# Layer-0 scores taken from x with joined weights, masks on GpSimd, and a reordered front and middle, in a two-layer graph kernel

## The chip, the cores and the metric

The kernel runs on one core of one Trainium2 chip, in float32 throughout. The metric is the device time of one launch in microseconds (us), the median of three runs. The engines are named as in the profile: PE (TensorE matmul), PEld (its weight load), DVE (VectorE), ACT (ScalarE), POOL (GpSimd), SP (SyncE, which here only issues DMAs).

## What is computed

There are 16 batches of N = 1024 nodes with D = 128 features, x and a dense adjacency matrix adj of zeros and ones, symmetric, with ones on its diagonal. Two layers follow each other, each with a residual and a layer norm. Cut to what matters:

```python
# layer 0
h = x @ Ww.T + Wb
e = (h @ A) @ h.T ;  e = e + e.T                 # = h (A + A.T) h.T
scores = where(adj > 0, e, 0)
attention = softmax(scores, axis=1) * adj
hp = relu(attention @ h)
ic, fc, oc = (sigmoid(hp @ w_u + x @ w_x) for each gate)
x = layernorm(x + oc * tanh(ic * hp + fc * x))
# layer 1, 4 heads
h = x @ conv_w + conv_b
Ah = tanh(adj * (h @ attn_w @ h.T))
hh = relu(Ah @ h)                                # per head
x = layernorm(x + relu(relu(mean over heads of hh) + x))
```

## The kernel before, in words

Features lie on the 128 partitions in the transposed tensors (xT, hT, gT, hpT, x1T, uT: 128 x 1024), nodes in the others. A block of 128 nodes against all 1024 nodes is one 128 x 1024 tile; each is made as two matmuls of 128 x 512 (q = 0, 1), and each such matmul is two passes of TensorE in the profile, so "x4" in the trace is one tile.

Nothing is rescheduled by a planner: every engine runs its own queue in the order in which the code emits instructions. That order is written by hand. A batch of layer 1 has 32 **steps**, numbered here 0 to 31 as `hd * NB + m` (head times 8 plus block). A step m of `layer1_step` issues two score matmuls (L358), the two multiplications with adj on DVE (L359) and one tanh on ACT (L360). The two matmuls that add the tile to the head's output (L364, "back") are kept in a queue and issued DELAY = 2 steps later. After a head's last block the output is added to a running sum on DVE (L374 and L376), which falls in the second step of the next head, and the next head's first accumulation must wait for that.

Layer 0 of the next batch, `layer0(b + 1)`, is a generator that runs inside these steps: at each step listed in BETWEEN one part of it is issued, up to its next `yield`. BETWEEN holds steps 1 to 27 without step 4. The last stage of the batch before, `layer1_end(b - 1)`, is a second generator: its first part is issued in step 3 (transposes L386, y on DVE L389 and L393, the statistics of `layernorm` L157 to L161 on DVE and the power on POOL L162) and its second part in step 4 (normalisation L165 on DVE, output DMA L395 on the POOL queue). Within a step the order is: layer 1, then the part of `layer1_end`, then the part of `layer0`.

So layer 0 in the kernel before runs as: step 1 hT (`project_T`), step 2 h with three gate columns (L218, L219), step 3 gT = a_sym hT (`project_T`, L174), then `front(j)` in step 5 + 2j and `middle(j)` with `back(j - 1)` in step 6 + 2j, the last `back` and the relu in step 21, gates in 22, u in 23 (L297 to L305), L311 and the statistics in 24, normalisation in 25.

`front(j)`: two score matmuls (L236), mask and multiply on DVE (L237), row maximum on DVE (L242), exp on ACT (L244), multiplication with adj on POOL (L245). `middle(j)`: the reciprocal of the sums (L252) and hz = h / sums (L254), both on DVE. `back(j)`: two accumulating matmuls (L260).

For batch 0 there is no layer 1 to run beside, so its layer 0 runs alone at the start of the kernel (the prologue).

PSUM has two accumulators of 128 x 1024 and one pool `ps_sc` of four 128 x 512 buffers under one tag, "sc". Every other PSUM tile (layer 1 scores, layer 0 scores, projections, transposes) takes the next of these four in turn, so each waits until the tile four places before it has been read. In SBUF the layer-0 tiles `s0` have three buffers, and adj tiles 17.

Of the kernel before, what the change touches and what calls it, by code (L numbers as in the profile page):

```python
# [10 lines left out]
F32 = mybir.dt.float32  # L11
AF = mybir.ActivationFunctionType
ALU = mybir.AluOpType
# [3 lines left out]
P = 128  # L17
# [4 lines left out]
def two_layer_adjacency_kernel(  # L22
# [19 lines left out]
    nc = tc.nc  # L42
    B, N, D = x.shape
    H = conv_w.shape[0]
    assert D == P and N % 512 == 0
    NB = N // P
# [3 lines left out]
    consts = ctx.enter_context(tc.tile_pool(name="consts", bufs=1))  # L50
    adjp = ctx.enter_context(tc.tile_pool(name="adjp", bufs=2 * NB + 1))
    sb = ctx.enter_context(tc.tile_pool(name="sb", bufs=2))
# [4 lines left out]
    def small(name):  # L57
        return ps_sc.tile([P, 512], F32, tag="sc", name=name)


    ident = consts.tile([P, P], F32, name="ident")
# [4 lines left out]
    ww_in = consts.tile([P, P], F32, name="ww_in")  # L66
    nc.sync.dma_start(ww_in, Ww)
    a_in = consts.tile([P, P], F32, name="a_in")
    nc.sync.dma_start(a_in, A)
    wb_col = consts.tile([P, 1], F32, name="wb_col")  # L70
    nc.sync.dma_start(wb_col, Wb.rearrange("(d o) -> d o", o=1))

    G = D + 3
    KG = 512 // G
    GROUPS = [range(k, min(k + KG, NB)) for k in range(0, NB, KG)]
    wwT_g = consts.tile([P, G], F32, name="wwT_g")
    ident_g = consts.tile([P, G], F32, name="ident_g")
    wwT = wwT_g[:, :D]
    nc.gpsimd.tensor_copy(ident_g[:, :D], ident)
    wb_row = consts.tile([P, G], F32, name="wb_row")  # L80
    nc.gpsimd.memset(wb_row[:, D:G], 0.0)
    nc.sync.dma_start(wb_row[:, :D], Wb.partition_broadcast(P))
    gate_u, gate_x = ident_g[:, D:G], wwT_g[:, D:G]

    for t, ws in ((gate_x, (wi_x, wf_x, wo_x)), (gate_u, (wi_u, wf_u, wo_u))):
        for g, w in enumerate(ws):
# [20 lines left out]
    caT = consts.tile([P, H, P], F32, name="caT")  # L107
    ms = consts.tile([P, H, P], F32, name="ms")

    a_sym = consts.tile([P, P], F32, name="a_sym")  # L110
    pw = small("pw")
    nc.tensor.transpose(pw[:, :P], ww_in, ident)
    nc.tensor.transpose(pw[:, P : 2 * P], a_in, ident)
    nc.scalar.copy(wwT, pw[:, :P])
    nc.vector.tensor_add(a_sym, pw[:, P : 2 * P], a_in)

    def join_weights():

# [51 lines left out]
    def project_T(dst, w, src, bias, name):  # L170

        for q in range(NH):
            ps = small(f"pT_{name}_{q}")
            nc.tensor.matmul(ps, w, src[:, ts(q, 512)], start=True, stop=True)  # L174
            if bias is None:
                nc.scalar.copy(dst[:, ts(q, 512)], ps)  # L176
            else:
                nc.scalar.activation(dst[:, ts(q, 512)], ps, AF.Identity, bias=bias)
# [13 lines left out]
    adj_t, x_t, x1_t = {}, {}, {}  # L192


    def layer0(b):

        xTb = sb.tile([P, N], F32, tag="xT", name=f"xT_{b}")
        nc.sync.dma_start(xTb, xT[b])
        adj_t[b] = []
        for j in range(NB):  # L200
            t = adjp.tile([P, N], F32, tag="adj", name=f"adj_{b}_{j}")
            nc.sync.dma_start(t, adjT[b, ts(j, P), :])
            adj_t[b].append(t)
            if j == 0:
                xb = sb.tile([P, NB, D], F32, tag="x", name=f"x_{b}", bufs=1)
                nc.sync.dma_start(xb, x[b].rearrange("(k p) d -> p k d", p=P))
                if b == 0:
                    load_late_weights()

        hT = sb.tile([P, N], F32, tag="hT0", name=f"hT0_{b}", bufs=1)  # L210
        gT = sb.tile([P, N], F32, tag="gT0", name=f"gT0_{b}", bufs=1)
        h = sb.tile([P, NB, G], F32, tag="h0", name=f"h0_{b}", bufs=1)
        project_T(hT, wwT, xTb, wb_col, f"h0_{b}")
        yield
        for ks in GROUPS:
            ps = small(f"pR_h0_{b}_{ks[0]}")[:, : len(ks) * G].rearrange("p (k d) -> p k d", d=G)
            for i, k in enumerate(ks):
                nc.tensor.matmul(ps[:, i, :], xTb[:, ts(k, P)], wwT_g, start=True, stop=True)  # L218
            nc.vector.tensor_add(  # L219
                h[:, ks[0] : ks[-1] + 1, :], ps,  # L220
                wb_row.unsqueeze(1).to_broadcast([P, len(ks), G]),
            )
        yield

        project_T(gT, a_sym, hT, None, f"g0_{b}")
        yield

        acc = ps_acc.tile([P, N], F32, tag="acc0", name=f"acc0_{b}")
        held = {}

        def front(j):

            s = sb.tile([P, N], F32, tag="s0", name=f"s0_{b}_{j}", bufs=3)
            for q in range(NH):
                ps = ps_sc.tile([P, 512], F32, tag="sc", name=f"sc0_{b}_{j}_{q}")
                nc.tensor.matmul(ps, hT[:, ts(j, P)], gT[:, ts(q, 512)], start=True, stop=True)  # L236
                nc.vector.scalar_tensor_tensor(  # L237
                    s[:, ts(q, 512)], adj_t[b][j][:, ts(q, 512)], 0.0, ps,
                    op0=ALU.is_gt, op1=ALU.mult,
                )  # L240
            nmax = sb.tile([P, 1], F32, tag="nmax", name=f"nmax_{b}_{j}", bufs=4)
            nc.vector.tensor_reduce(nmax, s, AX.X, ALU.max, negate=True)  # L242
            z = sb.tile([P, 1], F32, tag="z", name=f"z_{b}_{j}", bufs=4)
            nc.scalar.activation(s, s, AF.Exp, bias=nmax, accum_out=z)  # L244
            nc.gpsimd.tensor_mul(s, s, adj_t[b][j])  # L245
            held[j] = s, z

        def middle(j):

            s, z = held[j]  # L250
            rz = sb.tile([P, 1], F32, tag="rz", name=f"rz_{b}_{j}", bufs=4)
            nc.vector.reciprocal(rz, z)  # L252
            hz = sb.tile([P, D], F32, tag="hz", name=f"hz_{b}_{j}", bufs=4)
            nc.vector.tensor_scalar_mul(hz, h[:, j, :D], rz)  # L254
            held[j] = s, hz

        def back(j):
            s, hz = held.pop(j)
            for q in range(NH):
                nc.tensor.matmul(  # L260
                    acc[:, ts(q, 512)], hz, s[:, ts(q, 512)],
                    start=(j == 0), stop=(j == NB - 1),
                )


        for j in range(NB):
            front(j)
            yield
            middle(j)
            if j:  # L270
                back(j - 1)
            yield
        back(NB - 1)

        hpT = sb.tile([P, N], F32, tag="hpT", name=f"hpT_{b}", bufs=1)
        for q in range(NH):
            nc.scalar.activation(hpT[:, ts(q, 512)], acc[:, ts(q, 512)], AF.Relu)
        yield


        hp = sb.tile([P, NB, G], F32, tag="hp", name=f"hp_{b}", bufs=1)
        for ks in GROUPS:
            pt = small(f"pt0_{b}_{ks[0]}")[:, : len(ks) * G].rearrange("p (k d) -> p k d", d=G)
            for i, k in enumerate(ks):
                nc.tensor.matmul(pt[:, i, :], hpT[:, ts(k, P)], ident_g, start=True, stop=True)  # L285
            nc.scalar.copy(hp[:, ks[0] : ks[-1] + 1, :], pt)

        gate = sb.tile([P, NB, 3], F32, tag="gate", name=f"gate_{b}")
        gflat = gate.rearrange("p k g -> p (k g)")
        nc.vector.tensor_add(gate, hp[:, :, D:G], h[:, :, D:G])  # L290
        nc.scalar.activation(gflat, gflat, AF.Exp, scale=-1.0)
        nc.vector.tensor_scalar_add(gflat, gflat, 1.0)
        nc.vector.reciprocal(gflat, gflat)
        yield

        u = sb.tile([P, NB, D], F32, tag="u", name=f"u0_{b}", bufs=1)
        nc.gpsimd.tensor_mul(u, xb, gate[:, :, 1:2].to_broadcast([P, NB, D]))  # L297
        for q in range(NH):
            for i in range(BH):
                k = q * BH + i  # L300
                nc.vector.scalar_tensor_tensor(  # L301
                    u[:, k, :], hp[:, k, :D], gate[:, k, 0:1], u[:, k, :],
                    op0=ALU.mult, op1=ALU.add,
                )
            nc.scalar.activation(  # L305
                u[:, q * BH : (q + 1) * BH, :], u[:, q * BH : (q + 1) * BH, :], AF.Tanh
            )
        yield

        for k in range(NB):  # L310
            nc.vector.scalar_tensor_tensor(  # L311
                u[:, k, :], u[:, k, :], gate[:, k, 2:3], xb[:, k, :], op0=ALU.mult, op1=ALU.add
            )

        x1 = sb.tile([P, NB, D + 1], F32, tag="x1", name=f"x1_{b}")
        nc.gpsimd.memset(x1[:, :, 0:1], 1.0)
        yield from layernorm(u, x1[:, :, 1 : D + 1], f"0_{b}")
        x1_t[b] = x1
# [77 lines left out]


    first, join = layer0(0), None
    for step, _ in enumerate(first):
        if step == 3:  # L400
# [80 lines left out]
```

## Time and profile before

| what | value |
|---|---|
| median of three runs | 2664.63 us (2664.5 to 2665.58) |
| the profiled execution | 2664.39 us, its span 2662.6 us |
| PE busy | 2581.3 us, 97% of the span |
| DVE busy | 1650.3 us, 62% |
| ACT busy | 961.5 us, 36% |
| POOL busy | 402.0 us, 15% |
| chain that ended last | PE 86%, DVE 6%, issue 2%, POOL 1%, ACT 1% |

The span is the time from the first to the last instruction of the profiled execution. The chain that ended last is followed back from the last instruction, at each step to what released it. A busy PE is not PE at its peak, since the ends of matmuls are modelled, so the step from one matmul to the next in the chain is the better price of a matmul than the "mean ns of one".

### The profile page before, as it was taken

Reading aid. Unit: us, or ns where it says so; the run is one execution under the profiler, and the core shown is the slowest. Engines: PE = TensorE matmul, PEld = TensorE weight load, DVE = VectorE, ACT = ScalarE, POOL = GpSimd, SP = SyncE. Lnnn points to the kernel's source line nnn. Section 1 sums busy time; section 2 is a strip of 40 time slices with the busy share of each in tenths; the row PEclk is TensorE's granted clock in tenths of the full one; section 3 lists DMA queues with packets and bytes.
Section 4 is the critical chain, followed back from the end, with each engine's and each line's share of the span. In section 5 each row is a group of like instructions: output and inputs, shape, how many; then the busy total and the mean of one; then the engine's idle time right before and its main releaser. Section 6 shows DMA issues by size and latency. Waiting matters only on the chain.

```text
span 2662.6 us, 19095 instructions
## 1 busy us (share of the span) xinstructions
PE 2581.3 (97%) x6552; PEld 1187.3 (45%) x6552; DVE 1650.3 (62%) x2994; ACT 961.5 (36%) x1253; POOL 402.0 (15%) x219
## 2 busy tenths in 40 slices
PE   6799999999999999999999999999999999999997
PEld 3344444444444444444444444444444444444443
DVE  5475765747666575665747757476565756657454
ACT  2334334343333333333343343433333343333432
POOL 2120110202112021120201102021120211202000
PEclk9899999999999999999999999999999999999999
DMA  3202001020110202002020010201102020020000
GB/s 106 79 0 79 9 29 58 1 79 8 54 34 0 79 8 71 16 0 87 0 79 8 24 63 0 79 8 48 40 0 79 8 72 16 0 71 0 0 8 8
DMA packets 42264, 94.23 MB, mean 35 GB/s; under 512 B 3894, under 2 KB 21686, under 8 KB 42167
## 3 DMA queue, kind: packets, MB, share of 16 engines
q1 hardware_dynamic: 38999, 84.62, 9.7%
q0 software_dynamic: 2304, 8.39, 1.1%
q8 instruction: 51, 0.84, 0.1%
q14 instruction: 46, 0.38, 0.0%
q10 hardware_dynamic: 864, 0.00, 0.0%
HBM read 84.61 MB, written 8.39 MB: 35 GB/s over the span
## 4 chain that ended last, share of the span: by engine, by line
PE 86%; DVE 6%; issue 2%; POOL 1%; ACT 1%; POOLq 0%
PE acc L364 29%; PE sc L358 28%; PE sc L236 8%; PE acc L260 8%; PE pT_u L174 4%; PE pR L337 4%; DVE s L359 1%; DVE u L301 1%; DVE u L311 1%; POOL u L297 1%; PE pR_h L218 1%; PE pT_g L174 1%; PE pT_h L174 1%; DVE st L157 1%; PE pt L285 1%
## 5 line engine op out<-in xcount | busy, mean ns | idle before, releaser
L359 DVE TENSOR_TENSOR s<-sc,adj 128x512 f32<-128x512 f32 x1024 | 687.1, 687 | 603.3 <-PE sc L358 588.1
L364 PE MATMUL acc<-s,h 128*128 128x512 f32 x2048 | 963.3, 593 | 26.4 <-DVE sum L376 26.4
L358 PE MATMUL sc<-uT,x1T 128*128 128x512 f32 x2048 | 962.5, 593 | 0.5 <-DVE s L359 0.5
L360 ACT ACTIVATE s<-s 128x1024 f32<-128x1024 f32 x512 | 541.2, 1057 | 1029.1 <-DVE s L359 1028.0
L364 PEld LDWEIGHTS acc<-s,h 128*128 128x128 f32 x2048 | 388.5, 190 | 520.4 <-issue 481.0
L358 PEld LDWEIGHTS sc<-uT,x1T 128*128 128x128 f32 x2048 | 386.4, 190 | 467.8 <-issue 417.9
L245 POOL TENSOR_TENSOR s<-s,adj 128x1024 f32<-128x1024 f32 x128 | 301.2, 2353 | 1006.4 <-ACT s L244 885.8
L244 ACT ACTIVATE s<-s,nmax 128x1024 f32<-128x1024 f32 x128 | 147.0, 1149 | 445.7 <-DVE nmax L242 445.7
L254 DVE TENSOR_SCALAR hz<-h,rz 128x128 f32<-128x128 f32 x128 | 270.3, 2111 | 4.5
L237 DVE SCALAR_TENSOR_TENSOR s<-adj,sc 128x512 f32<-128x512 f32 x256 | 172.1, 685 | 162.6 <-PE sc L236 152.3
L260 PE MATMUL acc<-s,hz 128*128 128x512 f32 x512 | 245.6, 603 | 12.6 <-DVE hz L254 12.5
L236 PE MATMUL sc<-gT,hT 128*128 128x512 f32 x512 | 240.7, 593 | 0.0
L162 POOL TENSOR_TENSOR rs<-rs,mhalf 128x8 f32<-128x8 f32 x32 | 52.8, 1651 | 1005.4 <-DVE rs L161 1005.4
L260 PEld LDWEIGHTS acc<-s,hz 128*128 128x128 f32 x512 | 98.0, 193 | 137.3 <-issue 121.0
L242 DVE TENSOR_REDUCE nmax<-s 128x1 f32<-128x1024 f32 x128 | 156.2, 1220 | 4.4
L236 PEld LDWEIGHTS sc<-gT,hT 128*128 128x128 f32 x512 | 97.8, 191 | 123.4 <-issue 122.2
L174 PE MATMUL pT_u<-x1T,ms 128*128 128x512 f32 x256 | 121.9, 599 | 0.0
L337 PE MATMUL pR<-cw,x1T 128*128 128x512 f32 x256 | 114.9, 593 | 0.0
L340 ACT COPY h<-pR 128x512 f32<-128x512 f32 x128 | 75.0, 586 | 48.6 <-PE pR L337 48.6
L376 DVE SCALAR_TENSOR_TENSOR sum<-acc,sum 128x512 f32<-128x512 f32 x96 | 61.7, 685 | 37.2 <-PE acc L364 37.2
L176 ACT COPY uT<-pT_u 128x512 f32<-128x512 f32 x128 | 71.3, 581 | 21.5 <-PE pT_u L174 21.5
L174 PEld LDWEIGHTS pT_u<-x1T,ms 128*128 128x128 f32 x256 | 49.1, 192 | 61.2 <-issue 53.3
(70 smaller groups left out, 868.3 us busy)
## 6 DMA issues: line engine op xcount, KB each, us to landing
adj<-in_adjT_dram SPq DMA_DIRECT2D x128, 512.0 KB, 3.7
xT<-in_xT_dram SPq DMA_DIRECT2D x16, 512.0 KB, 4.3
x<-in_x_dram SPq DMA_DIRECT2D x16, 512.0 KB, 4.3
out_dram<-y POOLq DMA_DIRECT2D x16, 512.0 KB, 3.9
aw<-in_L_gnn_attn_w_dram SPq DMA_DIRECT2D x1, 256.0 KB, 4.9
cw_in<-in_L_gnn_conv_w_dram SPq DMA_DIRECT2D x1, 254.0 KB
ww_in<-in_L_gnn_Ww_dram SPq DMA_DIRECT2D x1, 64.0 KB, 2.2
a_in<-in_L_gnn_A_dram SPq DMA_DIRECT2D x1, 64.0 KB, 2.4
```

Source lines behind the costliest of these rows:

```text
L174: nc.tensor.matmul(ps, w, src[:, ts(q, 512)], start=True, stop=True)
L236: nc.tensor.matmul(ps, hT[:, ts(j, P)], gT[:, ts(q, 512)], start=True, stop=True)
L237: nc.vector.scalar_tensor_tensor(s[:, ts(q, 512)], adj_t[b][j][:, ts(q, 512)], 0.0, ps, op0=ALU.is_gt, op1=ALU.mult,)
L242: nc.vector.tensor_reduce(nmax, s, AX.X, ALU.max, negate=True)
L245: nc.gpsimd.tensor_mul(s, s, adj_t[b][j])
L254: nc.vector.tensor_scalar_mul(hz, h[:, j, :D], rz)
L260: nc.tensor.matmul(acc[:, ts(q, 512)], hz, s[:, ts(q, 512)], start=(j == 0), stop=(j == NB - 1),)
L337: nc.tensor.matmul(ps, x1T_t[b][:, ts(k, P)], cw.rearrange("p h d -> p (h d)"), start=True, stop=True)
L358: nc.tensor.matmul(ps, x1T[:, ts(m, P)], uT[:, ts(q, 512)], start=True, stop=True)
L359: nc.vector.tensor_mul(s[:, ts(q, 512)], ps, adj[:, ts(q, 512)])
L360: nc.scalar.activation(s, s, AF.Tanh)
L364: nc.tensor.matmul(acc[:, ts(q, 512)], h1[:, ts(hd, D)], s[:, ts(q, 512)], start=(m == 0), stop=(m == NB - 1),)
```

## The change

Layer 0's scores are written as x Q x.T with Q = Ww.T (A + A.T) Ww and two bias terms. With c = Ww.T (A + A.T) Wb, the part that runs along the columns goes into qT = Q xT + c as a bias per partition, and the part that is one number per row (c.x + Wb.(A + A.T)Wb) is carried as a fourth extra column of h. Q and c are made once, in the prologue, with two more rounds of small matmuls. hT and gT go; qT is the only projected transpose.

In the scores the mask is no longer made in the DVE instruction. `mask(j)` makes it on POOL, as adj > 0 into the tile s itself, and DVE then computes (scores + row number) * mask. `mask(0)` is emitted with `front(0)`; `mask(j + 1)` is emitted inside `front(j)`, ahead of the POOL multiplication of tile j. `front(j + 1)` is emitted ahead of `middle(j)`. hz is made on ACT in place of DVE. s0 has four buffers, hpT shares the buffer of qT.

Because the gT part is gone, layer 0 now runs one part earlier: step 1 qT, step 2 h, step 3 `mask(0)` and `front(0)`, then `front(j)` in step 3 + 2j for j of 1 and more, `middle(j)` in step 6 + 2j (the last in step 19), the last `back` and the relu in step 20, gates in 21, u in 22, L311's work in 23, normalisation in 24. BETWEEN is as it was.

```diff
-    G = D + 3
+    G = D + 4
...
+    nc.gpsimd.memset(ident_g[:, D:G], 0.0)
...
-    gate_u, gate_x = ident_g[:, D:G], wwT_g[:, D:G]
+    gate_u, gate_x = ident_g[:, D : D + 3], wwT_g[:, D : D + 3]
...
-    nc.tensor.transpose(pw[:, :P], ww_in, ident)
-    nc.tensor.transpose(pw[:, P : 2 * P], a_in, ident)
-    nc.scalar.copy(wwT, pw[:, :P])
-    nc.vector.tensor_add(a_sym, pw[:, P : 2 * P], a_in)
+    nc.tensor.transpose(pw[:, :P], a_in, ident)
+    nc.tensor.transpose(pw[:, P : 2 * P], ww_in, ident)
+    nc.vector.tensor_add(a_sym, pw[:, :P], a_in)
+    nc.scalar.copy(wwT, pw[:, P : 2 * P])
+    nc.vector.tensor_copy(b_wide, wb_col.to_broadcast([P, P]))
+    pw2 = small("pw2")
+    nc.tensor.matmul(pw2[:, :P], a_sym, ww_in, start=True, stop=True)
+    nc.tensor.matmul(pw2[:, P : P + 1], a_sym, wb_col, start=True, stop=True)
+    nc.vector.tensor_copy(s_ww, pw2[:, :P])
+    nc.vector.tensor_copy(sb_col, pw2[:, P : P + 1])
+    pw3 = small("pw3")
+    nc.tensor.matmul(pw3[:, :P], s_ww, ww_in, start=True, stop=True)
+    nc.tensor.matmul(pw3[:, P : P + 1], s_ww, wb_col, start=True, stop=True)
+    nc.tensor.matmul(pw3[:, P + 1 : P + 2], b_wide, sb_col, start=True, stop=True)
+    nc.vector.tensor_copy(q_w, pw3[:, :P])
+    nc.vector.tensor_copy(c_col, pw3[:, P : P + 1])
+    nc.vector.tensor_copy(wwT_g[:, G - 1 : G], pw3[:, P : P + 1])
+    nc.vector.tensor_copy(wb_row[:, G - 1 : G], pw3[:, P + 1 : P + 2])
...
-        hT = sb.tile([P, N], F32, tag="hT0", name=f"hT0_{b}", bufs=1)
-        gT = sb.tile([P, N], F32, tag="gT0", name=f"gT0_{b}", bufs=1)
+        qT = sb.tile([P, N], F32, tag="qT0", name=f"qT0_{b}", bufs=1)
...
-        project_T(hT, wwT, xTb, wb_col, f"h0_{b}")
+        project_T(qT, q_w, xTb, c_col, f"q0_{b}")
...
-        project_T(gT, a_sym, hT, None, f"g0_{b}")
-        yield
-
...
+        def mask(j):
+
+            s = sb.tile([P, N], F32, tag="s0", name=f"s0_{b}_{j}", bufs=4)
+            nc.gpsimd.tensor_scalar(s, adj_t[b][j], 0.0, None, ALU.is_gt)
+            held[j] = s
+
         def front(j):
 
-            s = sb.tile([P, N], F32, tag="s0", name=f"s0_{b}_{j}", bufs=3)
+            s = held[j]
...
-                nc.tensor.matmul(ps, hT[:, ts(j, P)], gT[:, ts(q, 512)], start=True, stop=True)
+                nc.tensor.matmul(ps, qT[:, ts(j, P)], xTb[:, ts(q, 512)], start=True, stop=True)
                 nc.vector.scalar_tensor_tensor(
-                    s[:, ts(q, 512)], adj_t[b][j][:, ts(q, 512)], 0.0, ps,
-                    op0=ALU.is_gt, op1=ALU.mult,
+                    s[:, ts(q, 512)], ps, h[:, j, G - 1 : G], s[:, ts(q, 512)],
+                    op0=ALU.add, op1=ALU.mult,
                 )
...
             nc.scalar.activation(s, s, AF.Exp, bias=nmax, accum_out=z)
+            if j + 1 < NB:
+                mask(j + 1)
             nc.gpsimd.tensor_mul(s, s, adj_t[b][j])
...
-            nc.vector.tensor_scalar_mul(hz, h[:, j, :D], rz)
+            nc.scalar.mul(hz, h[:, j, :D], rz)
...
+        mask(0)
+
+
+        front(0)
+        yield
         for j in range(NB):
-            front(j)
-            yield
+            if j + 1 < NB:
+                front(j + 1)
+                yield
             middle(j)
             if j:
                 back(j - 1)
             yield
         back(NB - 1)
 
-        hpT = sb.tile([P, N], F32, tag="hpT", name=f"hpT_{b}", bufs=1)
+        hpT = sb.tile([P, N], F32, tag="qT0", name=f"hpT_{b}", bufs=1)
...
-        nc.vector.tensor_add(gate, hp[:, :, D:G], h[:, :, D:G])
+        nc.vector.tensor_add(gate, hp[:, :, D : D + 3], h[:, :, D : D + 3])
```

## The prediction

> **What bounds the kernel now.** I read the page first, then the windows of single batches, then the timeline of the steps that the change touches. The page's slices and chain, and the three groups that the change moves or queues behind:
>
> ```profile
> PE   6799999999999999999999999999999999999997
> ...
> PE 86%; DVE 6%; issue 2%; POOL 1%; ACT 1%; POOLq 0%
> ...
> L245 POOL TENSOR_TENSOR s<-s,adj 128x1024 f32<-128x1024 f32 x128 | 301.2, 2353 | 1006.4 <-ACT s L244 885.8
> ...
> L254 DVE TENSOR_SCALAR hz<-h,rz 128x128 f32<-128x128 f32 x128 | 270.3, 2111 | 4.5
> ...
> L162 POOL TENSOR_TENSOR rs<-rs,mhalf 128x8 f32<-128x8 f32 x32 | 52.8, 1651 | 1005.4 <-DVE rs L161 1005.4
> ```
>
> After the first two slices PE never leaves 9. One batch period in the windows (us, PE, PEld, DVE, ACT, POOL, clock, DMA):
>
> ```profile
> 1392.70:1554.50 161.80, 160.04 (x409) 73.70 (x408) 103.04 (x187) 59.88 (x79) 25.04 (x13) 1.00 0.11 36
> ```
>
> PE is idle 1.76 us in 161.8, all in one place: the last head's first accumulation waits for the sum (L376). So a batch is a row of matmuls, at 1.72 us per tile of two 512-wide ones (the chain, from one tile to the next). A matmul removed is time saved; DVE, ACT and POOL cost nothing until they hold PE up. The timeline of steps 3 to 5, where the change puts its first mask:
>
> ```profile
> 1411.37 1.88 PE L174 MATMUL pT_g<-hT,a_sym 128*128 128x512 f32 x4
> ...
> 1415.94 0.17 DVE L161 TENSOR_SCALAR rs<-mv 128x8 f32<-128x8 f32 x1
> 1416.02 1.29 DVE L359 TENSOR_TENSOR s<-sc,adj 128x512 f32<-128x512 f32 x2
> 1416.19 1.64 POOL L162 TENSOR_TENSOR rs<-rs,mhalf 128x8 f32<-128x8 f32 x1 [52.13 <-DVE rs L161]
> 1416.52 1.88 PE L358 MATMUL sc<-uT,x1T 128*128 128x512 f32 x4
> 1417.86 2.14 DVE L165 TENSOR_SCALAR y<-y,mv,rs 128x128 f32<-128x128 f32 x8 [0.55 <-POOL rs L162]
> ```
>
> Start, duration, engine. Today POOL's power lies under two layer-1 multiplications: only L165 waits for it, 0.55 us. PE at 1416.52 already begins step 5; it is a full step ahead of DVE.
>
> **What the skill says.** "SBUF — State Buffer", section "Who interferes with whom": VectorE's two-port forms (tensor_scalar among them) and GpSimd exclude each other for a whole instruction, and whichever began first keeps the port. The trace agrees: hz (L254) takes 0.29 us at its shortest and 2.28 at the median, and one that began 0.86 us into a POOL multiplication ended 0.08 us after it (1426.10 + 1.57 against 1425.24 + 2.35). "GPSIMD Engine Reference", section 3.1, gives a two-input operation 2.6 cycles an element at 1.2 GHz, which is 2.22 us for 1024; L245 shows 2.35, so 0.13 are fixed. It gives a simple one-input body 1.03 cycles; no run here shows a one-input operation of that size.
>
> **The change, part by part.**
>
> *gT goes.* Batches 1 to 15 each lose one tile of matmuls: 15 x 1.72 = **25.8 us off**. The two 128x131 groups (1.79 us each a batch) grow by 1/131: 16 x 2 x 0.014 = 0.4 on. Together **-25.4**. One ACT copy pair goes, and is off the path.
>
> *hz to ACT.* It frees DVE of 270 us and costs ACT 128 x about 0.27 (the 128x128 copy at L114 took 0.265). DVE was not the bound in those steps (front and multiplications take 1.28 + 1.22 + 1.29 of 5.15 us). On ACT hz waits for the reciprocal, which DVE does right behind the multiplications of the same step, so the tanh behind hz is held some 0.3 us; its matmul comes two steps later. Price 0; if that cover went, ACT's late tanh would show on PE.
>
> *The prologue.* Here DVE, ACT and POOL set the pace, a tile every 6.2 us (L237 pair, maximum, exp, then hz blocked by POOL), from the landing of the second adj tile to the last L245:
>
> ```profile
> 26.95 1.28 DVE L237 SCALAR_TENSOR_TENSOR s<-adj,sc 128x512 f32<-128x512 f32 x2 [2.44 <-DMA adj<-in_adjT_dram]
> ...
> 68.55 2.34 POOL L245 TENSOR_TENSOR s<-s,adj 128x1024 f32<-128x1024 f32 x1 [3.96 <-ACT s L244]
> ```
>
> The SP queue is unchanged, so the second tile still lands at 26.9, and the weights' longer chain and front(0) disappear ahead of it (q_w is ready by about 7 from the rows of pw and a_sym, and xT lands at 8.9). From there the mask of tile j to its POOL multiplication takes 1.27 + 1.20 + 1.42 = 3.9 us (L237, L242, L244 with its wait), and POOL does one mask (M) and one L245 a tile. With M = 1.2 a tile takes 3.9 and the last multiplication ends near 57 instead of 70.9: **-14**. With M = 2.35 a tile takes 4.7 and it ends at 63.8: -7.
>
> *M.* Bounds: 1.03 cycles plus 0.13 gives an estimate of 1.0 us from the skill; the POOL 128x128 copy (0.287, L79) less 0.13, times 8, plus 0.13 gives 1.4; the two-input row gives 2.35. I take **1.2**.
>
> *mask(0) behind the power.* For batches 1 to 14 of layer 1 (14 times), step 3 now holds the end of the batch before and then mask(0) and front(0). The POOL queue has L162 and then mask(0); DVE has L161 and then front(0)'s multiplication, which waits for mask(0). Behind that wait on DVE stand L242, the multiplications of step 4, L165, and those of step 5. Step by step on the clock of the fence above: power ends 1417.83, mask(0) 1419.06, first DVE half 1419.8. PE's first matmul of step 5 takes the "sc" buffer of front(0)'s first half (four places before), so it starts at 1419.93 instead of 1416.52: **3.4 us** of stall (2.2 + M). PE then has two tiles of layer 1 and front(1)'s, 5.15 us, and comes to pT_u, whose buffer is freed by the first multiplication of step 5. DVE gets there after 1.28 + 1.2 + 1.28 + 2.1 + 0.7 from 1419.1, at 1425.5 against 1425.1: **0.6 more** with restart. But L165 (two-port) starts at 1422.7, and POOL's multiplication of tile 0 at 1422.98 (maximum's end plus 1.42): if POOL gets the port after the first of the eight, L165 ends 2.4 us later and this stall is **3.0**. No row shows who wins; I take the middle, 1.8. So 5.2 a batch, 14 x 5.2 = **+72.8**.
>
> *The later tail.* With everything one step earlier, L165 of layer 0 (2.14) comes ahead of the sum that PE waits for, but gates come 1.72 us of matmuls and a step sooner. Walked through with the same rows, PE's wait at the sum stays within 0.5 us of 1.76. Price 0, bound 15 x 0.5 = 7.5 either way. s0's fourth buffer, hpT in qT's place and xT held until step 17 meet no wait in the walk: SP's next xT stands behind adj tiles that come free only in step 31.
>
> **Sum.** 2664.4 (the profiled execution; span 2662.6 and 1.8 around it) - 25.4 - 14 + 72.8 = 2697.8. The median is 0.2 above that execution: **2698 us**, 1.3% slower. A measurement of this kernel tells about 0.2%, 5 us, from no change.
>
> **Rivals.** (1) *PE does not stall in step 5*: only the removed matmuls and the shorter prologue count: 2664.6 - 39.4 = 2625. For it: PE was full in these very steps, and DVE is idle a third of the time. Against it: the order of the queues, and that PE's lead is four buffers, no more. It decides where the stall per batch falls below 39.4 / 14 = 2.8 us; the first wait alone is 2.2 + M, so POOL would have to make a mask in 0.6. (2) *The stall is larger*: M as the two-input row, POOL taking the port, and PE slowed after the gap. "TensorE: Matmul & The Clock Gate", Part 1, says that an idle window of about 3.4 us halves the clock; the trace of before has both: after 2.6 us idle at 52.23 four passes took 1.96 us, after 2.6 at 58.51 they took 3.62, 1.7 more. Then 2.2 + 2.35 + 3.0 + 1.7 = 9.25 a batch, 129.5 - 25.4 - 7 = +97: 2762. (3) *The masks do not run as written*, say s0 buffers late so that mask(j + 1) holds POOL: the buffer comes from back(j - 3), one step before on PE, so I give this nothing beyond (2).
>
> **How the numbers follow.** The stall near my size 0.77, rival (1) or part of it 0.13, rival (2) 0.10. The main case's own bounds: M = 1.0, L165 first, prologue -15, tail -7: 14 x 3.8 - 47.4 = +6, 2670; M = 1.4, POOL first, half of the slow restarts: 14 x 7.4 - 39 = +65, 2730, with the tail's 7.5 on top 2737. Range 2664 to 2737. Faster 0.13, within 0.2% 0.07 (mostly the low end of the main case), slower 0.80.
>
> **What would show it.** In the changed profile: PE idle some 3.4 us before the first score matmul of step 5 of batches 1 to 14, released by DVE's masked multiplication, that one by POOL's mask, that one by the power; a second wait before pT_u; L165 there at 2.1 us in all or 4.5 (who has the port); POOL's mask row near 1.2 us; layer 1 beginning about 14 us sooner; the sum's wait still near 1.8. I am wrong if PE stays full in step 5, if masks take over 2 us, or if the batch period falls below 161.8.

## The result, and the profile after

The changed kernel takes **2737.76 us** (median of four runs, 2737.67 to 2738.02); the kernel before, on the same chip, 2665.11. The ratio is 1.0273, with a 95% interval of 1.0255 to 1.029: 72.7 us slower, where 33 were forecast. It lies just above the range that the prediction gave, 2664 to 2737. The profiled execution took 2738.02 us, its span is 2736.3.

From the page of the changed kernel, the row of the masks (busy us, mean ns of one, then the idle time ahead of them):

```profile
L253 POOL TENSOR_SCALAR s<-adj 128x1024 f32<-128x1024 f32 x128 | 354.0, 2769 | 41.2 <-DMA adj<-in_adjT_dram 22.8
```

A mask on POOL takes **2.77 us**, not the 1.2 that I had taken. PE's slices on the page are those of before, digit for digit: a slice is 68 us here and a 9 stands for 90% or more, so a stall of 5 us does not show in it. The chain that ended last covers only 4% of this trace, so nothing can be read from it. The waits of PE tell more (us in all, times, longest); first the one long wait of the steady steps before, then those after:

```profile
PE acc L364 <- DVE sum L376: 26.4, 15, 1.8
```

```profile
PE sc L390 <- DVE s L262: 66.2, 14, 4.7
PE acc L396 <- DVE sum L408: 19.5, 15, 1.3
...
PE pT_u L197 <- DVE s L391: 8.3, 11, 1.1
```

The wait of layer 1's score matmuls (L390, L358 before) is new: 14 times 4.73 us, released by the masked multiplication on DVE (L262). The wait for the sum (L396, L364 before) has shrunk. The third is new too: pT_u is the PSUM tile of the projection uT for the next head, which PE makes in step 5. The windows, over all but 0.4 us of one batch period (columns as before):

```profile
1424.00:1591.00 167.00, 160.15 (x405) 73.10 (x404) 88.79 (x179) 60.45 (x85) 47.10 (x21) 0.99 0.11 35
```

A period is the time from the first `y<-pt` of one batch to that of the next: 161.82 us before, **167.42** after, with four passes fewer. PE's busy time has not fallen by the removed tile's 1.72 us, since four passes a batch now take 3.65 us in place of 1.88, at a granted clock of 0.50; a restart of this kind is called **slow** below. The timeline of the steps in which that happens, in the middle of the kernel (start, duration, engine; the wait in brackets):

```profile
1450.32 1.64 POOL L185 TENSOR_TENSOR rs<-rs,mhalf 128x8 f32<-128x8 f32 x1 [56.07 <-DVE rs L184]
1451.94 5.50 POOL L253 TENSOR_SCALAR s<-adj 128x1024 f32<-128x1024 f32 x2
...
1454.74 1.41 DVE L262 SCALAR_TENSOR_TENSOR s<-sc,h,s 128x512 f32<-128x512 f32 x2 [4.50 <-POOL s L253]
...
1455.55 3.65 PE L390 MATMUL sc<-uT,x1T 128*128 128x512 f32 x4 [4.72 <-DVE s L262]
...
1458.51 4.29 DVE L188 TENSOR_SCALAR y<-y,mv,rs 128x128 f32<-128x128 f32 x8
...
1458.82 2.36 POOL L272 TENSOR_TENSOR s<-s,adj 128x1024 f32<-128x1024 f32 x1 [1.38 <-ACT s L269]
...
1463.46 1.98 PE L197 MATMUL pT_u<-x1T,ms 128*128 128x512 f32 x4 [0.82 <-DVE s L391]
```

Read it downwards. The power (L185) ends at 1451.96; only then does POOL make mask(0), and mask(1) right behind it. DVE's masked multiplication waits 4.50 us for mask(0), and PE's first score matmul of step 5 waits 4.72 us for DVE, as its PSUM buffer is free only then. Then L188 (L165 before) takes 4.29 us in place of 2.14, because POOL's multiplication began 0.31 us behind it. At pT_u PE waits again, 0.82 us. (PE would have begun step 5 at 1450.66, 1.72 us behind the tile that began at 1448.94, so the delay is 4.89 us for an idle time of 4.72.) This is the chain that the prediction named, in its place, with larger numbers.

The prologue, in the timeline: the last multiplication on POOL, and the normalisation of batch 0:

```profile
64.88 2.35 POOL L272 TENSOR_TENSOR s<-s,adj 128x1024 f32<-128x1024 f32 x1 [1.81 <-ACT s L269]
...
85.21 4.10 DVE L188 TENSOR_SCALAR x<-u,mv,rs 128x128 f32<-128x128 f32 x8 [1.79 <-POOL rs L185]
```

The last multiplication ends at 67.2 instead of 70.9, and L188 takes 4.10 us, since POOL already makes batch 1's masks. The first score matmul of layer 1 comes at 100.2 instead of 103.0: 2.8 us sooner, not 14. The figure is not the same wherever this prologue runs: e1_fill and e11_mul below have it too and begin layer 1 at 97.4. About half of that difference is the clock (the last eight accumulating passes took 5.37 us here and 4.03 there), and 0.8 us is the landing of the second adj tile.

### The profile page after: what moved, and what is told of

It reads as the page before. It is cut to its first block, busy times and chain, and to the rows that moved or that the text cites. A ratio compares the mean times of both kernels' runs of the same rounds, so it can differ in the third digit from the quotient of the medians.

```text
span 2736.3 us, 19441 instructions
## 1 busy us (share of the span) xinstructions
PE 2588.1 (95%) x6498; PEld 1181.5 (43%) x6498; DVE 1421.8 (52%) x2873; ACT 977.7 (36%) x1349; POOL 754.7 (28%) x348
## 5 line engine op out<-in xcount | busy, mean ns | idle before, releaser
L391 DVE TENSOR_TENSOR s<-sc,adj 128x512 f32<-128x512 f32 x1024 | 691.8, 688 | 895.2 <-PE sc L390 852.3
L390 PE MATMUL sc<-uT,x1T 128*128 128x512 f32 x2048 | 986.0, 605 | 66.7 <-DVE s L262 66.2
L396 PE MATMUL acc<-s,h 128*128 128x512 f32 x2048 | 968.8, 596 | 19.5 <-DVE sum L408 19.5
L390 PEld LDWEIGHTS sc<-uT,x1T 128*128 128x128 f32 x2048 | 391.4, 193 | 553.8 <-issue 412.7
L396 PEld LDWEIGHTS acc<-s,h 128*128 128x128 f32 x2048 | 391.9, 192 | 524.4 <-issue 489.3
L253 POOL TENSOR_SCALAR s<-adj 128x1024 f32<-128x1024 f32 x128 | 354.0, 2769 | 41.2 <-DMA adj<-in_adjT_dram 22.8
L185 POOL TENSOR_TENSOR rs<-rs,mhalf 128x8 f32<-128x8 f32 x32 | 52.9, 1653 | 1075.8 <-DVE rs L184 1075.8
L262 DVE SCALAR_TENSOR_TENSOR s<-sc,h,s 128x512 f32<-128x512 f32 x256 | 185.7, 746 | 211.2 <-PE sc L261 121.4
L261 PE MATMUL sc<-xT,qT 128*128 128x512 f32 x512 | 240.6, 593 | 0.0
L261 PEld LDWEIGHTS sc<-xT,qT 128*128 128x128 f32 x512 | 96.4, 191 | 116.3 <-issue 108.3
L329 POOL TENSOR_TENSOR u<-x,gate 128x1024 f32<-128x1024 f32 x16 | 30.5, 1906 | 251.4 <-DVE gate L325 251.4
```

The source lines that it names most:

```text
L253: nc.gpsimd.tensor_scalar(s, adj_t[b][j], 0.0, None, ALU.is_gt)
L261: nc.tensor.matmul(ps, qT[:, ts(j, P)], xTb[:, ts(q, 512)], start=True, stop=True)
L262: nc.vector.scalar_tensor_tensor(s[:, ts(q, 512)], ps, h[:, j, G - 1 : G], s[:, ts(q, 512)], op0=ALU.add, op1=ALU.mult,)
L390: nc.tensor.matmul(ps, x1T[:, ts(m, P)], uT[:, ts(q, 512)], start=True, stop=True)
L391: nc.vector.tensor_mul(s[:, ts(q, 512)], ps, adj[:, ts(q, 512)])
L396: nc.tensor.matmul(acc[:, ts(q, 512)], h1[:, ts(hd, D)], s[:, ts(q, 512)], start=(m == 0), stop=(m == NB - 1),)
```

## The experiments

Three questions were open. Is the loss the mask's **duration**, its **place** behind the power, or `front(0)`'s place in step 3? Does PE's slow restart add to the stall, or does it lie under DVE's work? And does POOL's extra work cost anything elsewhere? In short (us; the second column has the steps of layer 1 in which mask(0) and front(0) are issued; period and start of layer 1 as above; the waits are of PE per batch, in the step 5 scores and at pT_u). Each ratio is to executions of the kernel before that were taken beside that run (medians 2665.1 to 2666.3), so it need not be the quotient of two rows:

| kernel | mask(0), front(0) | time | ratio to before, 95% | layer 1 starts | period | wait sc / pT_u |
|---|---|---|---|---|---|---|
| before | - | 2664.6 | 1 | 103.0 | 161.8 | - |
| after | step 3, step 3 | 2737.8 | 1.0255 to 1.029 | 100.2 | 167.4 | 4.7 / 0.8 |
| e1_fill | 3, 3, PE kept busy | 2741.7 | 1.0268 to 1.0298 | 97.4 | 167.4 | 1.3 / 2.5 |
| e2_copy | 3 (a copy), 3 | 2722.8 | 1.0194 to 1.0228 | 92.2 | 165.7, 167.4 | 3.0 / 2.1 |
| e3_adj | none, 3 | 2677.0 | 1.0026 to 1.0056 | 89.0 | 162.8, 164.5 | 0 / 2.5 |
| e4_late | 2, 5 | 2646.9 | 0.9915 to 0.9944 | 99.9 | 161.0 | 0 / 0.6 |
| e5_early | 2, 3 | 2733.9 | 1.0243 to 1.0273 | 97.4 | 167.3 | 0 / 2.7 |
| e6_adj_late | none, 5 | 2634.7 | 0.9869 to 0.9902 | 87.4 | 160.9 | 0 / 0.5 |
| e7_hz_dve | e6 with hz on DVE | 2633.7 | 0.9868 to 0.9897 | 87.0 | 160.9 | 0 / 0.5 |
| e8_uT | e6, pT_u one step later | 2619.9 | 0.9816 to 0.9845 | 87.2 | 160.0 | 0.5 in step 6 |
| e9_tail | e8 without step 24 | 2613.3 | 0.9786 to 0.9816 | 87.7 | 159.5 | 0.5 in step 6 |
| e10_step4 | none, 4 | 2640.9 | 0.9888 to 0.9921 | 89.4 | 161.3 | 0 / 0.5 |
| e11_mul | 3 (a product), 3 | 2735.4 (one run) | - | 97.4 | 167.4 | 4.7 / 0.8 |
| e12_front5 | 3, 5 | 2663.7 | 0.9984 to 1.0001 | 98.0 | 162.2 | 0 / 1.8 |

e3 and e6 to e10 multiply by adj itself, which is its own mask because it holds only zeros and ones; the comparison with 0 is what they leave out.

### e1_fill: PE given work across the first stall

```diff
+    def filler(b):
+        for _ in range(2):
+            for q in range(NH):
+                nc.tensor.matmul(
+                    acc0_t[b + 1][:, ts(q, 512)], ident, x1T_t[b][:, ts(q, 512)],
+                    start=True, stop=True,
+                )
...
+                if nxt is not None and end is not None and hd == 0 and m == 4:
+                    filler(b)
```

> The changed kernel with two extra tiles of matmuls (four of 128x512, results discarded) issued at the end of step 4, so that PE has 3.4 us of work in its 4.7 us gap before step 5. Nothing else changes. Theory A (the DVE queue sets the end of the whole stretch: front(0) waits for mask(0), then maximum, step 4's multiplications, the normalisation and step 5's first multiplication, which frees the buffer of pT_u): the slow restart goes (four passes 1.9 us in place of 3.65), but the wait before pT_u grows from 0.8 to about 2.5 us, and the time stays within 6 us of 2738. Theory B (the halved clock after the gap is a cost of its own): 14 x 1.77 = 25 us less, 2713.

Measured: 2741.7 us; the period is unchanged at 167.4, but for three batches that are 1.4 to 1.7 us longer. The timeline of PE, step 5's first tile and pT_u:

```profile
448.38 1.98 PE L399 MATMUL sc<-uT,x1T 128*128 128x512 f32 x4 [1.30 <-DVE s L271]
...
456.29 1.98 PE L197 MATMUL pT_u<-x1T,ms 128*128 128x512 f32 x4 [2.49 <-DVE s L400]
```

The gap shrinks from 4.72 to 1.30 us and the tile behind it runs in 1.98 us, not 3.65. What is won there, 1.67 us, comes back as wait at pT_u: 2.49 instead of 0.82. So after the first stall it is DVE's chain that sets when PE goes on. **The slow restart was real and cost nothing**; the second stall is the longer DVE chain, however PE spends the time. The three longer batches are those in which the four passes at pT_u took 2.43, 3.43 and 2.48 us in place of 1.98: a slow restart there has nothing to hide it.

### e2_copy and e11_mul: the mask's duration

```diff
-            nc.gpsimd.tensor_scalar(s, adj_t[b][j], 0.0, None, ALU.is_gt)
+            nc.gpsimd.tensor_copy(s, adj_t[b][j])
```

(e2_copy; e11_mul has `tensor_scalar(s, adj_t[b][j], 1.0, None, ALU.mult)` there, the same form of instruction with another operation.)

> The changed kernel with the mask made by a plain GpSimd copy of adj (which holds only zeros and ones) in place of the comparison; same tile, same place, same queues. It measures a one-input POOL operation of 128x1024. Theory A: every us that mask(0) gets shorter comes off the step-5 stretch of 14 batches and off each prologue tile while POOL sets its pace; if the copy takes 1.4 us in place of 2.77: 14 x 1.37 + 8 = 27 less, about 2711; if it takes 1.0: about 2703. Rival (any one-input operation of that size on POOL costs as much as the comparison): copy near 2.8, time 2738.

> The changed kernel with the mask made as adj * 1.0 by the same GpSimd tensor_scalar instruction in place of adj > 0. If the comparison is what makes the mask 2.77 us, this takes about 1.0 to 1.1 as the copy does; if the tensor_scalar form is, it stays at 2.8.

The group of each, e2 first, then e11:

```profile
L253 POOL COPY s<-adj 128x1024 f32<-128x1024 f32 x128 | 132.1, 1038 | 41.9 <-DMA adj<-in_adjT_dram 23.6 <-issue 17.5 <-PE pt L360 0.7
```

```profile
L253 POOL TENSOR_SCALAR s<-adj 128x1024 f32<-128x1024 f32 x128 | 354.3, 2771 | 40.4 <-DMA adj<-in_adjT_dram 22.1 <-issue 17.9
```

The copy takes 1.04 us; the product by 1.0 takes 2.77, as the comparison does. The cost belongs to the form of the instruction (`tensor_scalar`), not to comparing. PE's waits in e2:

```profile
PE sc L390 <- DVE s L262: 41.5, 14, 3.0
PE pT_u L197 <- DVE s L391: 27.4, 13, 2.5
```

The first stall falls from 4.73 to 2.96, by 1.77 for a mask that is 1.73 shorter: it is the mask's duration plus 1.9, built as the prediction built it. Yet the whole fell by 14.9 us only, 8.0 of that in the prologue (5.2 if e1's and e11's start of layer 1 is taken). I had expected 2703 to 2711. Periods come in two kinds, 165.7 (four of them) and 167.35 (nine), and the timeline of PE tells why: a batch of each kind, step 5's first tile and pT_u:

```profile
439.57 2.74 PE L390 MATMUL sc<-uT,x1T 128*128 128x512 f32 x4 [2.97 <-DVE s L262]
...
447.47 1.98 PE L197 MATMUL pT_u<-x1T,ms 128*128 128x512 f32 x4 [0.78 <-DVE s L391]
...
2442.82 1.99 PE L390 MATMUL sc<-uT,x1T 128*128 128x512 f32 x4 [2.97 <-DVE s L262]
...
2450.72 3.43 PE L197 MATMUL pT_u<-x1T,ms 128*128 128x512 f32 x4 [2.48 <-DVE s L391]
```

The gap ahead of step 5 is 2.97 us in both. In the first batch the slow restart comes behind it, and pT_u is reached 7.90 us later; in the second there is none, and pT_u is reached 7.90 us later as well, DVE's time again. But then the gap at pT_u is 2.48 us, the slow restart comes there, and the period is 1.7 us longer. One restart costs nothing in the one place and its full price in the other.

### e3_adj: no mask made at all

```diff
-            nc.gpsimd.tensor_scalar(s, adj_t[b][j], 0.0, None, ALU.is_gt)
...
-                    s[:, ts(q, 512)], ps, h[:, j, G - 1 : G], s[:, ts(q, 512)],
+                    s[:, ts(q, 512)], ps, h[:, j, G - 1 : G], adj_t[b][j][:, ts(q, 512)],
```

> The changed kernel without masks: front multiplies by adj itself (zeros and ones), so POOL has no mask and nothing waits for one; front(0) stays in step 3. Theory A: the wait for the mask goes, but front(0) still stands on DVE ahead of the normalisation (L188), and POOL's multiplication of tile 0 still comes about 0.3 us after L188 began and takes the port: pT_u waits some 3 us, per batch +3.1 - 1.7 - 0.5 = +0.9; with the prologue 14 us shorter: about 2662. Rival B (the mask's place behind the power is the whole cause): no wait is left, 2618 to 2625. Rival C (POOL's load as such slows DVE and PE everywhere): about 2620 as well, but then the kernel with masks placed elsewhere stays above 2700.

Measured: 2677.0, against 2662 expected. The wait for the mask is gone. The second stall is still there, from the timeline:

```profile
1254.48 4.27 DVE L188 TENSOR_SCALAR y<-y,mv,rs 128x128 f32<-128x128 f32 x8
...
1254.78 2.36 POOL L271 TENSOR_TENSOR s<-s,adj 128x1024 f32<-128x1024 f32 x1 [2.27 <-issue]
...
1259.41 3.46 PE L197 MATMUL pT_u<-x1T,ms 128*128 128x512 f32 x4 [2.48 <-DVE s L390]
```

`front(0)` in step 3 sends POOL's multiplication into L188, and PE waits 2.48 us at pT_u (34.6 us over 14 batches). What I missed is the 3.46: in 9 of 14 batches this gap too is followed by slow passes (3.32 to 3.67), in 5 by 1.98, and the periods are 164.5 and 162.8. Nothing stands behind this restart to hide it; 9 x 1.7 = 15 us is the miss.

### e10_step4: front(0) one step later, behind L188

```diff
-    BETWEEN = set(range(1, 28)) - {4}
+    BETWEEN = set(range(1, 28)) - {3}
```

(e3 with this line.)

> e3_adj with front(0) in step 4 in place of step 3, so that on DVE it stands behind L188 and POOL's multiplication of tile 0 comes after L188 instead of 0.3 us into it. DVE has the same instructions before the one that frees pT_u's buffer as in e3_adj. Theory (POOL takes the port from L188): L188 2.1 us in place of 4.3, the wait before pT_u 2.5 - 2.1 = 0.4 to 1.2 us, no slow restart (1.7 us in about two of three batches), together about 2.5 to 3 a batch: 2677 - 40 = 2637. Rival (the amount of DVE work ahead of step 5 is what costs, not the port): no change, 2677.

Measured: 2640.9, 36 us below e3, where 40 were expected. DVE does the same work in the same two steps, in another order. The timeline:

```profile
1237.29 2.14 DVE L188 TENSOR_SCALAR y<-y,mv,rs 128x128 f32<-128x128 f32 x8 [0.56 <-POOL rs L185]
...
1242.65 1.98 PE L197 MATMUL pT_u<-x1T,ms 128*128 128x512 f32 x4 [0.53 <-DVE s L390]
```

L188 is back at 2.14 us and the wait at 0.53. So the second stall was POOL's multiplication taking the port from L188, not the amount of DVE work.

### e4_late, e5_early, e12_front5: the two places apart

```diff
-        yield
-
         acc = ps_acc.tile([P, N], F32, tag="acc0", name=f"acc0_{b}")
...
         mask(0)
-
-
+        yield
+        yield
         front(0)
```

(e4_late: mask(0) in step 2, front(0) in step 5. e5_early has one of the two new `yield`s, so front(0) stays in step 3. e12_front5 keeps the `yield` ahead of `acc` and has one behind mask(0): mask(0) in step 3, front(0) in step 5. In e4 and e12 all later parts of layer 0 move with front(0).)

> The changed kernel with all its masks on POOL, mask(0) issued in step 2 (ahead of the power) and front(0) in step 5, so that steps 3 and 4 hold only layer 1 and the end of the batch before; the other fronts two steps later too. Theory A (place): no wait in step 5, PE full, L188 2.1 us in all, period 161.8 - 1.7 = 160.1; with the prologue as in the changed kernel (3 us less than before): 2664.6 - 25.4 - 3 = 2636. Rival C (the load of the masks on POOL, 354 us, and on the port shared with DVE, is what costs): stays above 2700.

> The changed kernel with mask(0) issued one step earlier, in step 2, ahead of the power in POOL's queue; front(0) stays in step 3, all masks stay on POOL. It separates the mask's place from front(0)'s place. If the mask's place behind the power is the whole cause, no wait is left: about 2630. Theory A now: the 4.7 us gap goes, but front(0) still stands ahead of L188 on DVE, and mask(1) and the multiplication of tile 0 follow each other on POOL from the end of the power: if POOL keeps the port through both, pT_u waits some 3.7 us and restarts slowly, +3.6 a batch, about 2710; if L188 gets in between them, 1.4 us, about 2656.

> The changed kernel with front(0) in step 5 and mask(0) left in step 3, behind the power in POOL's queue; masks as in the changed kernel. Nothing on DVE waits for mask(0) any more. If front(0)'s step is all that matters: as e4_late, 2647. Theory (the shared port): mask(0) begins as the power ends, the very moment at which L188 may start, and holds it 2.8 us; pT_u then waits 0.5 + 2.8 = 3.3 and restarts slowly: +3 to +5 a batch on e4_late, 2690 to 2715.

e4 takes 2646.9, 19 us below the kernel before, with every mask on POOL (expected 2636). Of PE's waits, the sum's is that of before (26.5 us in 15), and:

```profile
PE pT_u L197 <- DVE s L389: 7.8, 14, 0.6
```

These 7.8 us are a part of gT's saving that is lost: PE comes to pT_u 1.72 us sooner, and DVE's chain does not. In the kernel before, the buffer of pT_u was free some 1.1 us ahead of PE (1420.6 against 1421.7 in the batch whose steps the prediction shows), less than 1.72.

e5 takes 2733.9: moving the mask alone wins next to nothing. That refutes the theory that the mask's place is the whole cause (2630), and both figures of the other theory (2710 and 2656) are too low as well, since it did not count what follows. Its waits, and a stretch of its timeline near the tail of layer 0:

```profile
PE pT_u L197 <- DVE s L388: 37.6, 14, 2.7
PE acc L393 <- DVE sum L405: 36.7, 15, 2.5
```

```profile
1057.07 2.78 POOL L251 TENSOR_SCALAR s<-adj 128x1024 f32<-128x1024 f32 x1
1057.11 3.38 DVE L188 TENSOR_SCALAR x<-u,mv,rs 128x128 f32<-128x128 f32 x8 [0.60 <-POOL rs L185]
```

The 4.7 us are gone, but the port conflict of step 4 stays, now with the slow restart in the open (3.25 to 3.68 at pT_u in 13 of 14 batches). And a mask that stands ahead of the power no longer waits for step 3: POOL runs it in step 24 of the batch before, into the other L188 (x, the normalisation of layer 0), which makes the sum late: 2.54 us of wait, with a slow restart behind it. A second conflict has been added to the first.

e12 takes 2663.7, no different from before, and **74 us below the changed kernel by one `yield` ahead of front(0)**. I had expected 2690 to 2715. With front(0) in step 5 nothing on DVE queues behind the wait for the mask until PE is served, and mask(0) has two steps to be made in. POOL still works beside L188, but costs less than I thought; the timeline, and the eight instructions of L188 (ns: least, median, most):

```profile
440.49 2.77 POOL L253 TENSOR_SCALAR s<-adj 128x1024 f32<-128x1024 f32 x1
...
440.55 3.37 DVE L188 TENSOR_SCALAR y<-y,mv,rs 128x128 f32<-128x128 f32 x8 [0.53 <-POOL rs L185]
```

```profile
L188 DVE TENSOR_SCALAR y<-y,mv,rs x8: 329/335/1054, 440.6 to 443.6; 128x128 f32<-128x128 f32 x8
```

The first began 0.06 us into a POOL instruction of 2.77 and yet took only 1.05, the longest of the eight: this form doesn't hold the port for its whole length. The same query in the changed kernel, where POOL's two-input multiplication meets L188:

```profile
L188 DVE TENSOR_SCALAR y<-y,mv,rs x128: 332/335/2497, 286.7 to 2730.1; 128x128 f32<-128x128 f32 x128
```

There the longest took 2.50 us, which is the multiplication's 2.36 and a little. In e12 a wait of 1.76 us a batch remains at pT_u: 24.6 us in all, about what the removal of gT saves. The period is 0.3 us longer than before and layer 1 begins 5.0 us sooner; hence the zero.

### e6_adj_late and e7_hz_dve: the rest of the change with the stalls gone

e6 is e3 with the steps of e4. e7 also puts hz back:

```diff
-            nc.scalar.mul(hz, h[:, j, :D], rz)
+            nc.vector.tensor_scalar_mul(hz, h[:, j, :D], rz)
```

> No masks on POOL (adj itself is the mask) and front(0) in step 5: the two mended places together. Theory A: the period of e4_late (160.97 us, since PE's step 5 is the same) with the prologue of e3_adj (layer 1 begins at 89 in place of 99.9): 2647 - 11 = 2636. If masks on POOL cost anything in the steady steps as well (rival C in small), the period falls below e4_late's, and the time below 2630.

> e6_adj_late with hz back on DVE (the kernel before's instruction), so that only the move of hz to ACT is undone. My price for that move in the steady steps was 0. Expected: period unchanged, the prologue 2 to 6 us longer since hz is blocked by POOL's multiplication again: 2 to 6 above e6_adj_late. If hz on ACT had been a cost (tanh held behind it), this is faster than e6_adj_late.

e6 takes 2634.7, where 2636 were expected. Against e4 it is 12.3 us faster, and layer 1 begins 12.5 us sooner (87.4 against 99.9): all of it is the prologue, and POOL's masks cost nothing in the steady steps once they stand in the right place. e7 cannot be told from e6, where 2 to 6 us more had been expected. hz takes 0.48 us on DVE there in the mean, not 2.11 as before: with front ahead of middle it mostly no longer meets POOL's multiplication. The move of hz to ACT is worth nothing here.

### e8_uT and e9_tail: two steps towards a better kernel

```diff
-                elif m == NB - 3:
+                elif m == NB - 2:
                     head_uT(b, hd + 1)
...
-    BETWEEN = set(range(1, 28)) - {4}
+    BETWEEN = set(range(1, 28)) - {4, 24}
```

(The first is e8, on e6; both are e9.)

> e6_adj_late with the projection uT of the next head (L197, pT_u) issued in step 6 of a head in place of step 5. In e4_late PE waits 0.56 us before pT_u in step 5 of 14 batches: without gT, PE comes there 1.72 us sooner, and DVE's chain through the normalisation of the batch before does not. Theory (half of gT's saving is lost to that wait): the wait goes, 14 x 0.87 = 12 us less than e6_adj_late. Rival (the period of 160.97 has another cause): no difference from e6_adj_late.

> e8_uT with step 24 also left out for layer 0, so that its statistics fall in step 25 behind the sum, and its normalisation in step 26. In e8_uT PE still waits 0.8 us at the sum in 15 batches (and 0.5 before step 6 of 14). Theory (that wait is DVE's statistics ahead of the sum): it goes, 15 x 1 = 15 us less, about 2605. Rival (the normalised x comes too late for its transposes in step 28): a new wait there, no gain or a loss.

e8 gains 14.8 us, near the 12 expected, but from elsewhere. Its waits:

```profile
PE acc L393 <- DVE sum L405: 11.9, 15, 0.8
PE sc L387 <- DVE s L388: 7.4, 14, 0.5
```

The 7.4 us that I meant to take away stay and only move from pT_u to a score tile; the sum's wait fell from 26.4 to 11.9. That pT_u, one step later, keeps PE busy nearer to the sum is my reading of it; it was not tested apart. e9 takes that rest away too. The window of one period of e9:

```profile
419.00:578.53 159.53, 158.90 (x406) 72.66 (x405) 87.15 (x179) 61.21 (x85) 25.09 (x13) 1.00 0.11 37
```

e9 gains 6.6 us; the 15 expected were more than the 11.9 us of wait that e8 had left at the sum. PE is busy all but 0.63 of 159.53 us, 0.53 of which is the score wait, so there is hardly any idle time left in a period. **e9_tail, 2613.3 us, ratio 0.9801 (0.9786 to 0.9816), is faster than both kernels**, for an adj of zeros and ones.

## Why the prediction was right in direction and wrong in size

The profiled execution went from 2664.39 to 2738.02 us, +73.6, where the sum had +33.4. The mechanism held: the wait named, its place, its releasers and its 14 times. The reason given against rival (1), the order of the queues, held too. The 40 us between come from terms of the sum (the last column is what each adds to the forecast):

| term | predicted | measured | adds, us |
|---|---|---|---|
| first stall (2.2 + M), 14 times | 3.41 | 4.89 | +20.7 |
| second stall to pT_u, 14 times | 1.8 | 2.76 | +13.4 |
| prologue | -14 | -2.8 | +11.2 |
| sum's wait, 15 times | 0 | -0.46 | -6.9 |
| PE's four passes at pT_u, 14 times | 1.88 | 1.98 | +1.4 |

They add up to 39.8 of the 40.2. That the result came so near to the top of the range, 2737, is luck: the top was made of M at 1.4 us, half the cost of a slow restart that costs nothing, and 7.5 us for a longer wait at the sum, which got shorter.

- **M is the step that failed.** I took 1.2 us from the price of a one-input line-rate body ("GPSIMD Engine Reference", section 3.1) and from the copy of L79, and set 2.35, the two-input row, as the highest. It measured 2.77, above that bound; "if masks take over 2 us" was one of the prediction's own signs of being wrong. The copy in e2 (1.04) shows that my 1.0 was right for a copy: the error was to take a comparison for one. The same section's sentence covers a simple one-input body; e11 shows that `tensor_scalar` is not among them here. M enters twice: 14 x 1.57 in the first stall (less 14 x 0.09, as the rest was 2.1), and in the prologue.
- **The second stall** is the other term that was mis-sized. "POOL gets the port" was the right one of the two values (3.0), and the middle between them was taken; measured were 2.76. L188 took 4.29, near the 4.5 of that case. (The five DVE rows there add up to 1425.7, not 1425.5; the 0.6 us fits the former.) This agrees with "SBUF — State Buffer", section "Who interferes with whom", for the two-input multiplication. It does not for the mask in e12, where no instruction of L188 took over 1.05 us under a POOL instruction of 2.77.
- **The prologue.** The tile was to take 3.9 us. With M = 2.77 POOL alone needs 2.77 + 2.36 a tile, and is the bound. The six runs with no mask (e3, e6 to e10) begin layer 1 13.6 to 16.0 us sooner: the walk of the other engines was about right, and M was not. With a mask of 1.04 (e2) it is 10.8; 1.4 of the other 3 us are L188, which took 3.56 us under the next batch's copies, and the rest stays open. L188 in the prologue, 4.10 for 2.14 with the masks of this kernel, was not foreseen. Some 2.8 of the 11.2 us are not there in e1 and e11, whose prologue is the same.
- **The slow restart** was put in rival (2) as 1.7 us more. It comes behind each of the 14 first stalls (3.12 to 3.78 us), and e1 and e2 show that it adds nothing there. Rival (2)'s sum, 2762, counted it beside the second stall; in the kernel they lie under each other.
- **gT.** Its 25.4 us are right as work. But part of it had covered DVE's lag at pT_u: e4, with both stalls gone, has 7.8 us of wait there. "A matmul removed is time saved" was too simple; a removed matmul also takes away cover.
- **hz at 0** (e7), the buffers and the x transfers at 0: none shows in the waits of PE from layer 1 on. **The tail** was within its bound of 7.5, on the good side.

The kernel spends what it saved, and more, because `front(0)` entered the step just ahead of the two places where PE depends on DVE. Two steps later (e12) the same masks on the same engine give the time of before.

What decides whether a gap of about 2.5 us is followed by a slow restart can be read from the traces. "TensorE: Matmul & The Clock Gate", Part 1, says that the clock follows PE's activity in a window of 3413 ns that runs free of the kernel, and gives an idle window of about 3.4 us for the halving. The granted clock agrees with the first: between the start of layer 1 and the tail of the kernel it falls, in every run that has slow restarts, to 0.50 for one such window or two, and all of a run's stretches at half clock begin on one grid of 3.413 us. It does not ask for a whole idle window, though. Two windows of that grid in e3, each with the one behind it (columns as in the prediction); the gap at pT_u is 2.48 us in the first batch and 2.47 in the second:

```profile
1255.59:1259.00 3.41, 1.34 (x4) 0.27 (x2) 3.41 (x8) 0.13 (x1) 1.55 (x1) 1.00 0.00 0
1259.01:1262.42 3.41, 3.01 (x4) 1.46 (x5) 3.38 (x5) 1.06 (x1) 0.96 (x1) 0.50 0.52 154
...
1747.11:1750.52 3.41, 1.46 (x4) 0.38 (x2) 3.41 (x8) 0.24 (x1) 1.66 (x1) 1.00 0.00 0
1750.53:1753.94 3.41, 2.90 (x7) 1.43 (x8) 3.38 (x5) 1.06 (x1) 0.96 (x1) 1.00 0.50 149
```

PE is idle 2.07 us in the first window, and the next one is granted half the clock; it is idle 1.96 in the third, as the rest of that gap falls into the fourth, and the clock stays whole. In all the traces together 81 full-clock windows of that part are followed by one at half clock, and in each of them PE was idle for 2.01 us or more; in none of the others was it idle for over 2.02. So what counts is how much of a gap falls into one window, with the border at about 2.0 us. (e2 shows the grid at work: 49 of these windows are 167.25 us, 0.10 less than its longer period, and the passes at pT_u grow from 2.58 to 3.43 us over ten batches, by 0.09 to 0.10 at each.) At half clock a window that PE fills loses half of its 3.41 us, which is the 1.7 us of a slow restart.

## What to carry to other kernels

When a piece of work moves to an earlier step, list for each of its instructions what stands behind it in its queue, and which shared port its follow-on work takes; here the follow-on multiplication on POOL cost 36 us by itself (e3 against e10). Price an operation that the trace lacks by a row of the same form of instruction, and if there is none, let the bound go above the dearest row. Removing PE work brings PE earlier to every engine that feeds it, so look for the next wait before counting the whole saving.

## What the hardware showed that I had not expected

- On POOL a one-input `tensor_scalar` of 128 x 1024 float32 took 2.77 us, more than a two-input multiplication (2.36), whether it compares or multiplies; a copy took 1.04.
- POOL can take the shared port between two of DVE's back-to-back instructions: the longest of L188's eight took 2.50 us in place of 0.335. Under a POOL `tensor_scalar` (e12) none took over 1.05.
- A gap of 2.48 us on PE was followed by slow passes in 9 of e3's 14 batches and in 3 of e1's, gaps of 1.76 (e12) in none, gaps of 4.72 in all. About 2.0 us of idle time within one window of a fixed 3.413 us grid were enough to halve the clock in the next; a gap of 2.5 us escapes it where the grid divides it.
- DVE's masked multiplication with a number per row took 0.746 us for 128 x 512, against 0.69 for the plain multiplication of L391.
